# Four transformer blocks on one core: layer 0's spreads over two DMA queues, a limit on late pieces, a fifth early expert slot, and another order in the attention over heads

## Chip, core and metric

The kernel runs on one core of a Trainium2 chip. A core has TensorE (PE in the profile, with its weight loads PEld), VectorE (DVE), ScalarE (ACT), GpSimd (POOL) and SyncE (SP), each with an instruction stream of its own, in order. DMAs are issued from SP, ACT or POOL. The metric is the time of the kernel on the device in microseconds (us); smaller is better.

## The reference, cut to what matters

Four blocks work one after another on x (4 x 512 x 288, float32), all with layer norm, shift, scale and gates that are computed from a conditioning vector per batch, and 16 heads of 18 elements. Layers 1 and 3 differ from each other in nothing that matters here.

```python
# layer 0: attention over 512 tokens, then the best 2 of 4 experts per token
h = _modulate(_ln(x), sh_msa, sc_msa)
q, k, v = ...
attn = softmax(einsum('bhqd,bhkd->bhqk', q, k) * hd ** -0.5)
x = x + g_msa * (einsum('bhqk,bhkd->bhqd', attn, v) @ w_proj + b_proj)
xf = _modulate(_ln(x), sh_mlp, sc_mlp).reshape(-1, C)
topk_logits, topk_idx = top_k(xf @ w_gate, 2)
x = x + g_mlp * (sum over the two experts e of gates[e] * (gelu(xf @ w1[e] + b1[e]) @ w2[e] + b2[e]))
# layers 1 and 3: attention over tokens, then one MLP (288 -> 1152 -> 288)
# layer 2: attention over the 16 heads of each token, then one MLP
attn = softmax(einsum('nthd,ntkd->nthk', q * scale, k))       # 16 x 16 for each token
out = einsum('nthk,ntkd->nthd', attn, v)
out = out.transpose(0, 2, 1, 3).reshape(n, t, d)               # heads ahead of tokens
x = x + gate_msa * (out @ proj_w + proj_b)
```

## The kernel before

**One order, written by a planner.** The instructions of all engines are emitted in one order that the program works out itself. Around a backbone of loops stand lists of tasks: `products` (TensorE work), `lanes` (small DVE, ACT and POOL work), `moves` (scatters to memory), `loads`, `spreads` and `casts`. A task has a due time, keys that must be ready, and a generator that emits it piece by piece and yields the estimated cost of each piece. The planner's clock `flow["now"]` goes up by one at each `gap` (L152) of the backbone; it counts emission and not time. `fill` (L126) takes from a list what is ready, up to a budget in us; when the budget is used up it goes on as long as the open task, or the next, is past its due time (plus `SLACK`, 8, for lanes and moves). `mark(key, delay)` makes a key ready `delay` gaps later. A generator that yields `WAIT` gives up its turn until the next gap, one that yields `BANK` waits for a free bank of PSUM, and `Whole` marks the end of a unit of TensorE work.

**Two coroutine lists.** Where the stage of layer 2 runs beside the MLPs, `chain` (the tile loop) and `beside` (work next to it) are advanced by `follow` (L181) at each gap, against a credit that grows by 1.6 per gap. A bank that is free is offered to `beside` first and then to `chain` (L207).

**Token attention (layers 0, 1, 3).** Four batches times four units of four heads, 64 steps in all. Queries and keys come out of TensorE as packed rows `qc` (L640, ACT copy L666) and must be spread, so that each head starts at a partition of its own: `spread` (L686) issues one DMA for each head j and each half s (queries or keys), 19 rows of 512 elements, on SP, except the later heads of unit 0, which go out on ACT. Four buffers `spreads_of` rotate. A step computes scores (L711), takes their maximum on DVE (`mx`, L721), and six steps later (`LEAD`) the scores again, turned, with the exponential on ACT (`ex`, L749) and the product with the values (L777). `set_maxima` (L755) turns the maxima (L760), copies them on ACT (L762) and writes them into the unit's spread buffer by a DMA from POOL (L763). In the norm (L506) POOL computes the power for `rstd` (L528, or L520 to L523 where ACT does the scaling), and DVE (L543, L546, L548) or ACT (L537) scales. Each step ends with two gaps, in which the other tasks are emitted.

**Experts (layer 0).** When a batch's attention is done, `logits` (L1335) turns the normed rows `xh` (L1343) and multiplies them with the gate; then follow the choice of experts, places, and `scatter` (L1495), eight indirect DMAs from POOL (L1500) that write the rows to memory sorted by expert. The products run as 19 blocks of 256 rows (`expert_block`, L1690), each for one expert. The first `EARLY` (4) of them are blocks known to be full after two of the four batches, and load from a first list; the others need the list and the scatter of all batches. `SHORT` names two slots after them with 128 rows. `DONE` says after which block a batch's results can be gathered.

**Layer 2's attention over heads** runs on DVE, POOL and ACT beside the MLPs of layers 1 and 2. It goes over 16 tiles of 128 tokens (`stream`, L1153). For each tile, `kept` (L993) computes query, key and value by TensorE (L1002); the query stays in a bank, key and value images go to SBUF by ACT (L1011), into the first two thirds of the buffer `spreads_of[i % 4]`. `weigh` multiplies and sums on DVE (L1020, L1026), four groups a tile; the exponential is on ACT (L1193), `weighted` on POOL (L1039), `summed` on DVE (L1051), `finish` scales (L1064) and sends the result to memory. After four tiles `after` (L1130) reads the batch back with heads ahead of tokens, turns its rows (L1082), projects, and prepares the MLP's input; `before` (L1121) does the norm of the next batch. MLP work (L1916, gelu on ACT L1927, L1938) fills TensorE meanwhile.

Of the kernel before, what the change touches and what calls it, by code (L numbers as in the profile page):

```python
# [19 lines left out]
P = 128  # L20
# [30 lines left out]
INSIDE = (44, 56)  # L51
RATE = 1.6
SLACK = 8
EARLY = 4
SHORT = (EARLY + 1, EARLY + 3)
TRIOS = [[0, 1, 2], [3, 4, 5], [6, 7, 8]]
DUOS = [[0, 1], [2, 3], [4, 5], [6, 7], [8]]
# [3 lines left out]
def tile_dit_blocks(ctx: ExitStack, tc: tile.TileContext, x_in, cond_t, sel_den, sel_b, w_gate, layers, out):  # L61
# [25 lines left out]
    n_layers = len(layers)  # L87


    flow = {"now": 0, "turn": 0, "others": (6, 7), "credit": 0.0, "rate": 0.0}  # L90


    chain, beside = [], []
# [29 lines left out]
                return where.pop(i)  # L123
        return None

    def fill(where, started, us, slack=0):  # L126

        while True:
            if not started:
                item = take(where, us <= 0, slack)  # L130
                if item is None:
                    return us
                started.append(item)
            if us <= 0 and started[0][0] + slack > flow["now"]:
                return us
            try:
                took = next(started[0][2])
            except StopIteration:
                started.pop()
                continue  # L140
            if took is WAIT:
                return us
            us -= took

    def fill_others():
        fill(lanes, open_lane, 1.0, SLACK)
        fill(moves, open_move, 1.0, SLACK)
        fill(loads, open_load, 1000.0)
        fill(spreads, open_spread, 1000.0)
        fill(casts, open_cast, 1000.0)  # L150

    def gap(us):  # L152
        flow["now"] += 1
        before = flow["turn"]
        wanted = any(item[1] for item in chain + beside)
        fill(products, open_product, 0.0 if wanted else us)
        used = flow["turn"] != before or bool(open_product)
        fill_others()
        if chain or beside:
            close_all()  # L160
            follow(used)
# [22 lines left out]
    def follow(used):  # L184


        flow["credit"] = min(flow["credit"] + flow["rate"], 3.0)
        bank = [not used]

        def piece(item):  # L190
            if item[1]:
                if not bank[0]:
                    return False
                bank[0] = item[1] = False
            cost = next(item[0], None)
            if cost is None:
                (chain if item in chain else beside).remove(item)
                return False
            if cost is BANK:
                item[1] = True  # L200
                return piece(item)
            if cost is WAIT:
                return False
            flow["credit"] -= cost
            return True

        for item in beside + chain:  # L207
# [295 lines left out]
    xh, ht = {}, {}  # L503
    held = []

    def norm(l, half, b):  # L506
        key = (l, half, b)
        n = f"{l}_{half}_{b}"
        mv = small.tile([P, TB, 2], F32, tag="mv", name=f"mv_{n}")
# [7 lines left out]
        if scalar:  # L517

            off = small.tile([P, TB], F32, tag="off", name=f"off_{n}")
            nc.gpsimd.tensor_scalar_add(rstd, mv[:, :, 1], EPS)  # L520
            nc.gpsimd.tensor_tensor(rstd, rstd, minus_half, ALU.pow)
            nc.gpsimd.tensor_tensor(off, mv[:, :, 0], rstd, ALU.mult)
            nc.gpsimd.tensor_scalar_mul(off, off, -1.0)  # L523
            for _ in range(3):
                yield WAIT
        else:
            nc.vector.tensor_scalar_add(rstd, mv[:, :, 1], EPS)
            nc.gpsimd.tensor_tensor(rstd, rstd, minus_half, ALU.pow)  # L528
# [76 lines left out]
    def attention(l, start):  # L605
# [81 lines left out]
        def spread(u):  # L687

            b, g = divmod(u, NG)
            t = qk[u] = spreads_of[u % 4]  # L690
            for j in range(HG):
                for s in range(2):

                    at = g * UQ + (s * HG + j) * HO
                    end = at + HO
                    to = j * HP
                    while at < end:
                        m, r = divmod(at, P)
                        n = min(end - at, P - r)
                        queue = nc.scalar if u == 0 and j >= HG // 2 else nc.sync  # L700
                        queue.dma_start(t[to : to + n, s, :], packed[b, m][r : r + n, :])
# [136 lines left out]
        def steps(inside=None, tail=None):  # L838
# [9 lines left out]
            def sum_pair(step, to):  # L848
                sum_values(step - 1, to, True, False)
                sum_values(step, to, False, True)  # L850

            for step in range(first_step, N_STEPS + 1):
                odd = step % 2
                mark(("step", l, step), 0)
                if step < end:
                    flow["others"], flow["turn"] = ((4, 5, 6, 7) if odd and step > 0 else (0, 1, 2, 3)), -1
# [56 lines left out]
        for b in range(B):  # L913
# [3 lines left out]
            task(  # L917
                lanes, start - 70 if first else at_step(s0 - LEAD - 9 if b else s0 - LEAD - 6),
                [("x", l, 0, b)] + ([("scattered", B - 1)] if l == 1 else []) + ([("step", l, 0)] if b else []),
                norm(l, 0, b),  # L920
            )
            free = [("first products", l, b - 2)] if b >= 2 else []
            if prev == OVER_HEADS and b < 2:
# [58 lines left out]
    def attention_over_heads(l):  # L982
# [12 lines left out]
        def kept(i, s):  # L995

            b, t = tiles[i]
            h = ht[l, 0, b]
            to = QUERIES[i % 2][:, :C] if s == 0 else other()[:, :C]
            for k in range(NK):  # L1000
                n = KP + (1 if k == NK - 1 else 0)
                nc.tensor.matmul(  # L1002
                    to, h[:n, k, t * P : (t + 1) * P], w["wqkv"][:n, k, s * C : (s + 1) * C],
                    start=k == 0, stop=k == NK - 1,
                )
            if s == 1:
                qkv[i] = spreads_of[i % 4].rearrange("p s f -> p (s f)")[:, : 2 * C].rearrange(
                    "p (s h d) -> p s h d", s=2, d=HD
                )
            if s:  # L1010
                nc.scalar.activation(  # L1011
                    qkv[i][:, s - 1].rearrange("p h d -> p (h d)"), to, AF.Copy, scale=SCALE if s == 1 else 1.0
                )

        def weigh(i, g):
            hs = slice(g * GH, (g + 1) * GH)
            if g == 0:
                sc[i] = work.tile([P, NH, NH], F32, tag="hs", bufs=4, name=f"hs_{l}_{i}")
            prod = work.tile([P, GH, NH, HD], F32, tag="va", bufs=1, name=f"pq_{l}_{i}_{g}")
            nc.vector.tensor_tensor(  # L1020
                prod,
                QUERIES[i % 2][:, :C].rearrange("p (h d) -> p h d", d=HD)[:, hs, :].unsqueeze(2).to_broadcast([P, GH, NH, HD]),
                qkv[i][:, 0].unsqueeze(1).to_broadcast([P, GH, NH, HD]),
                ALU.mult,
            )
            nc.vector.tensor_reduce(sc[i][:, hs, :], prod, AX.X, ALU.add)  # L1026
# [7 lines left out]
        def weighted(i, g):  # L1034
# [4 lines left out]
            engine.tensor_tensor(  # L1039
                prod,  # L1040
                sc[i][:, hs, :].unsqueeze(2).to_broadcast([P, GH, HD, NH]),
                qkv[i][:, 1].rearrange("p h d -> p d h").unsqueeze(1).to_broadcast([P, GH, HD, NH]),
                ALU.mult,
            )
            pv[i, g] = prod
# [76 lines left out]
        def before(b):  # L1122

            yield from until(("x", l, 0, b))
            if b >= 2:
                yield from until(("first products", l, b - 2))
            yield from norm(l, 0, b)
            yield from turn_normed(0, b)

        def after(b):  # L1130
# [1 line left out]
            for _ in range(3 if b < B - 1 else 1):  # L1132
                yield WAIT
            read(b)
            for _ in range(6 if b < B - 1 else 3):
                yield WAIT
            yield from until(("gated", b))
            for k in range(NK):
# [3 lines left out]
            for t in range(TB):  # L1142
                yield BANK
                project(b, t)
                yield -1.5
            mark(("x", l, 1, b), 2)
            if b < B - 1:
                beside.append([gate_projection(b + 1), False])
            yield from until(("x", l, 1, b))
            yield from norm(l, 1, b)  # L1150
            yield from turn_normed(1, b)

        def stream():  # L1153
# [182 lines left out]
    def logits(b):  # L1336
        key = (0, 1, b)
        h = work.tile([P, NK, S], F32, tag="hm", bufs=4, name=f"hl_{b}")
        for k in range(KF + 1):
            n = P if k < KF else RC  # L1340
            to = other()
            for t in range(TB):
                nc.tensor.transpose(to[:n, t * P : (t + 1) * P], xh[key][:, t, k * P : k * P + n], ident)  # L1343
            nc.scalar.copy(h[:n, k, :], to[:n, :])
            yield Whole(0.43)
        pl = other()
        for k in range(KF + 1):
            n = P if k < KF else RC
# [147 lines left out]
    def scatter(b):  # L1496
        key = (0, 1, b)
        for t in range(TB):
            for s in range(2):
# [4 lines left out]
                unordered(i, "x_mem")  # L1504
                scatters.append(i)
                nc.gpsimd.memset(tick, 0.0)
                yield 0.5
        held.remove(key)
        mark(("scattered", b))

# [181 lines left out]
    def expert_block(i):  # L1692
# [517 lines left out]
```

## Time and profile before

| what | us |
|---|---|
| median of three runs (2243.33 to 2248.39) | 2246.33 |
| the profiled execution | 2245.67 |
| its span, first to last instruction | 2244.0 |
| TensorE busy | 2075.5 (92%) |
| DVE busy | 1066.5 (48%) |
| ACT busy | 815.7 (36%) |
| POOL busy | 503.7 (22%) |
| mean granted clock of TensorE | 0.961 |

The chain of work that ended last has 62% of the span on TensorE and 12% on DVE. In time, layer 0's attention takes about the first 440 us, the expert blocks the time to about 872, layer 1's attention to about 1290; layer 2's attention over heads runs from there to 1629 (its last L1064 at 1628.89), and the rest is the end of layer 2 and layer 3. An "idle before" in brackets at an instruction is the time that its engine stood still before it, with what released it.

### The profile page before, as it was taken

Reading aid. Unit: us, or ns where it says so; the run is one execution under the profiler, and the core shown is the slowest. Engines: PE = TensorE matmul, PEld = TensorE weight load, DVE = VectorE, ACT = ScalarE, POOL = GpSimd, SP = SyncE. Lnnn points to the kernel's source line nnn. Section 1 sums busy time; section 2 is a strip of 40 time slices with the busy share of each in tenths; the row PEclk is TensorE's granted clock in tenths of the full one; section 3 lists DMA queues with packets and bytes.
Section 4 is the critical chain, followed back from the end, with each engine's and each line's share of the span. In section 5 each row is a group of like instructions: output and inputs, shape, how many; then the busy total and the mean of one; then the engine's idle time right before and its main releaser. Section 6 shows DMA issues by size and latency. Waiting matters only on the chain.

```text
span 2244.0 us, 28773 instructions
## 1 busy us (share of the span) xinstructions
PE 2075.5 (92%) x10720; PEld 1159.9 (52%) x10720; DVE 1066.5 (48%) x1660; ACT 815.7 (36%) x1325; POOL 503.7 (22%) x516
## 2 busy tenths in 40 slices
PE   7899989889999998989999999979799999999998
PEld 2333434357777575344454466657556444444555
DVE  4556656632002403566534279798821355664111
ACT  2434433422222122545435422434312555546111
POOL 1101020231002203110000129788811201001010
PEclk9989998989999999999999999999899999999999
DMA  3244211425665453100000000210310100000000
GB/s 80 62 126 154 72 57 26 113 95 172 197 200 172 131 178 121 35 23 20 17 6 20 1 17 9 66 31 7 40 42 23 50 22 15 15 20 1 0 22 21
DMA packets 170957, 139.10 MB, mean 62 GB/s; under 512 B 79379, under 2 KB 152523, under 8 KB 170818
## 3 DMA queue, kind: packets, MB, share of 16 engines
q1 hardware_dynamic: 164670, 126.10, 19.6%
q0 software_dynamic: 5952, 10.85, 1.6%
q8 instruction: 85, 1.39, 0.3%
q14 instruction: 54, 0.44, 0.1%
q10 hardware_dynamic: 196, 0.31, 0.0%
HBM read 96.49 MB, written 26.00 MB: 55 GB/s over the span
## 4 chain that ended last, share of the span: by engine, by line
PE 62%; DVE 12%; issue 4%; DMA 3%; POOL 2%; ACT 2%; SPq 1%; another core or an unknown queue 0%; POOLq 0%; ACTq 0%; DVEq 0%
PE banks L711 11%; PE banks L640 7%; PE banks L1730 7%; PE banks L1710 6%; PE banks L1879 5%; PE banks L1856 4%; PE banks L777 4%; PE banks L828 3%; PE banks L1938 3%; DVE mx L721 3%; PE banks L1916 2%; DVE pq L1020 2%; DVE ho L1051 2%; DVE hs L1026 2%; DMA qk<-qc 1%
## 5 line engine op out<-in xcount | busy, mean ns | idle before, releaser
L721 DVE TENSOR_REDUCE mx<-banks 128x4 f32<-128x2048 f32 (+1 forms) x354 | 423.6, 1238 | 353.0 <-PE banks L711 310.3
L749 ACT ACTIVATE ex<-banks 128x1024 f32<-128x1024 f32 (+1 forms) x471 | 377.9, 865 | 318.2 <-PE banks L711 312.8
L711 PE MATMUL banks<-qk 32*128 32x512 f32 x3072 | 442.3, 634 | 39.9 <-DVE mx L721 19.2
L711 PEld LDWEIGHTS banks<-qk 32*128 32x128 f32 x3072 | 168.2, 187 | 218.0 <-issue 83.0
L777 PE MATMUL banks<-ex,va 128*32 128x512 f32 x1536 | 193.1, 616 | 2.7 <-ACT ex L749 2.5
L1039 POOL TENSOR_TENSOR pv<-hs,qk 128x1152 f32<-128x1152 f32 x60 | 190.6, 3192 | 8.0 <-ACT hs L1193 7.9
L1730 PE MATMUL banks<-w_b,hid_b 128*128 128x288 f32 x648 | 178.2, 418 | 0.0
L640 PE MATMUL banks<-ht,wqk 96*128 96x512 f32 (+1 forms) x348 | 167.7, 615 | 9.2 <-DVE mx L721 8.1
L1710 PE MATMUL banks<-block,w_b 128*128 128x256 f32 (+1 forms) x684 | 154.8, 372 | 0.6 <-ACT hid_b L1722 0.6
L1722 ACT ACTIVATE hid_b<-banks,b_b 128x256 f32<-128x256 f32 (+1 forms) x171 | 66.8, 461 | 241.2 <-PE banks L1716 134.5
L1730 PEld LDWEIGHTS banks<-w_b,hid_b 128*128 128x128 f32 x648 | 117.2, 190 | 49.8 <-issue 23.5
L1916 PE MATMUL banks<-ht,w 128*128 128x256 f32 x432 | 113.9, 396 | 25.7 <-ACT hid L1927 25.3
L1710 PEld LDWEIGHTS banks<-block,w_b 128*128 128x128 f32 x684 | 123.9, 192 | 25.2 <-issue 7.4
L1938 PE MATMUL banks<-w,hid 128*128 128x288 f32 x432 | 130.5, 436 | 0.0
L763 POOL DMA_DIRECT2D qk<-maxima x48 | 29.6, 617 | 446.3 <-ACT maxima L762 381.6
L640 PEld LDWEIGHTS banks<-ht,wqk 96*128 96x128 f32 (+1 forms) x348 | 61.4, 187 | 101.3 <-issue 57.9
L777 PEld LDWEIGHTS banks<-ex,va 128*32 128x32 f32 x1536 | 40.2, 111 | 140.7 <-issue 73.7
L599 POOL TENSOR_TENSOR x<-x,upd_a 128x288 f32<-128x288 f32 x48 | 38.6, 804 | 320.1 <-DVE upd_a L598 300.3
L1879 PE MATMUL banks<-w,hid 128*128 128x288 f32 x432 | 108.8, 410 | 0.0
L1916 PEld LDWEIGHTS banks<-ht,w 128*128 128x128 f32 x432 | 83.0, 197 | 46.4 <-ACT hid L1927 28.5
L596 DVE TENSOR_TENSOR upd_m<-banks,b 128x576 f32<-128x576 f32 x12 | 9.1, 754 | 205.9 <-PE banks L1879 205.9
L1856 PE MATMUL banks<-ht,w 128*128 128x512 f32 x216 | 100.4, 612 | 5.0 <-ACT hid L1872 4.5
(243 smaller groups left out, 2503.0 us busy)
## 6 DMA issues: line engine op xcount, KB each, us to landing
w_b<-in_w SPq DMA_DIRECT2D x57, 432.0 KB
w_b<-in_w SPq DMA_DIRECT2D x57, 384.0 KB
qk<-qc SPq DMA_DIRECT2D x316, 38.0 KB
wa<-in_wada SPq DMA_DIRECT2D x24, 288.0 KB
x_mem<-zeros SPq DMA_DIRECT2D x21, 256.0 KB
y_mem<-zeros SPq DMA_DIRECT2D x21, 256.0 KB
block<-x_mem SPq DMA_DIRECT2D x17, 288.0 KB
y_mem<-y_b SPq DMA_DIRECT2D x17, 288.0 KB
```

What stands on the lines that cost most here:

```text
L640: nc.tensor.matmul(to, st(rows, k), mv(rows, k), start=k == 0, stop=k == NK - 1)
L711: nc.tensor.matmul(to, qk[u][r, of, c * P : (c + 1) * P], qk[u][r, 1 - of, :], start=True, stop=True)
L721: nc.vector.tensor_reduce(mxs[u % 2][:, j : j + n, c], banks[:, bank + j : bank + j + n, :], AX.X, ALU.max)
L749: nc.scalar.activation(ex[step, j // 2][:, j % 2 : j % 2 + n, :], banks[:, to[j] : to[j] + n, :], AF.Exp, scale=SCALE)
L777: nc.tensor.matmul(to[j * HP : (j + 1) * HP, :], vas[0][:, c, at : at + HP], ex[step, j // 2][:, j % 2, :], start=first, stop=last,)
L1039: engine.tensor_tensor(prod, sc[i][:, hs, :].unsqueeze(2).to_broadcast([P, GH, HD, NH]), qkv[i][:, 1].rearrange("p h d -> p d h").unsqueez ...
L1710: nc.tensor.matmul(banks[:, UP + j, cols], w1[:, k, j * P : (j + 1) * P], hx[i][:, k, cols], start=k == 0, stop=False)
L1730: nc.tensor.matmul(banks[:, PY + t, :C], hid[j][:, t * P : (t + 1) * P], w2[:, j, :], start=f == 0, stop=f == NF - 1)
L1856: nc.tensor.matmul(banks[:, 4 + j, :], full[:, k, (f % 3) * P : (f % 3 + 1) * P], h[:, k, :], start=k == 0, stop=False,)
L1879: nc.tensor.matmul(banks[:, t, :C], hf[:, t * P : (t + 1) * P], w["w2"][f // 3][:, f % 3, :], start=f == 0, stop=f == NF - 1,)
L1916: nc.tensor.matmul(banks[:, UP + j, :BT], full[:, k, (f % 3) * P : (f % 3 + 1) * P], h[:, k, s], start=k == 0, stop=False,)
L1938: nc.tensor.matmul(banks[:, PY + t, :C], hf[:, t * P : (t + 1) * P], w["w2"][f // 3][:, f % 3, :], start=False, stop=f == NF - 1,)
```

## The change

Five parts. The first early expert slots are five and not four, which moves `SHORT` and `DONE` too. In layer 0, the half s = 1 of every spread goes out on POOL's queue. Lanes and moves that are late stop in a gap after 0.8 us over their budget in attention steps (`least`), until two steps before the end of the look-ahead; products that are late stop at 0.05 over it in expert blocks (`most`); a scatter is counted as 1.0 and the last batch's turned rows in `logits` as 0.6. In `follow`, the free bank is offered to `chain` first. In the over-heads stage key images lie in the first third of their buffer, value images in the second and third by turns of four tiles; the norm ahead of layer 3 waits 10 gaps between POOL and ACT instead of 3, that of layer 2's batches 2 and 3 waits 6; `after` waits 13 gaps (9 in the last batch) before it turns rows, where it was 6 (3); and the next batch's gated projection is taken up after the norm rather than ahead of it.

```diff
-EARLY = 4
+EARLY = 5
 SHORT = (EARLY + 1, EARLY + 3)
...
-    def fill(where, started, us, slack=0):
+    def fill(where, started, us, slack=0, least=-1e9):
...
-            if us <= 0 and started[0][0] + slack > flow["now"]:
+            if us <= least or us <= 0 and started[0][0] + slack > flow["now"]:
                 return us
...
-        fill(lanes, open_lane, 1.0, SLACK)
-        fill(moves, open_move, 1.0, SLACK)
+        fill(lanes, open_lane, 1.0, SLACK, flow["least"])
+        fill(moves, open_move, 1.0, SLACK, flow["least"])
...
-        fill(products, open_product, 0.0 if wanted else us)
+        fill(products, open_product, 0.0 if wanted else us, 0, flow["most"])
...
-        for item in beside + chain:
+        for item in chain + beside:
             if item[1]:
                 piece(item)
...
-    def norm(l, half, b):
+    def norm(l, half, b, lag=3):
...
-            for _ in range(3):
+            for _ in range(lag):
                 yield WAIT
...
-                        queue = nc.scalar if u == 0 and j >= HG // 2 else nc.sync
+                        queue = nc.scalar if u == 0 and j >= HG // 2 else nc.gpsimd if l == 0 and s else nc.sync
...
+            flow["least"] = -0.8
             for step in range(first_step, N_STEPS + 1):
                 odd = step % 2
+                if step == end - 2:
+                    flow["least"] = -1e9
...
-                norm(l, 0, b),
+                norm(l, 0, b, 10 if first and prev == OVER_HEADS else 3),
...
-            if s == 1:
-                qkv[i] = spreads_of[i % 4].rearrange("p s f -> p (s f)")[:, : 2 * C].rearrange(
-                    "p (s h d) -> p s h d", s=2, d=HD
-                )
             if s:
-                nc.scalar.activation(
-                    qkv[i][:, s - 1].rearrange("p h d -> p (h d)"), to, AF.Copy, scale=SCALE if s == 1 else 1.0
-                )
+                third = 0 if s == 1 else 1 + i // 4 % 2
+                mine = spreads_of[i % 4].rearrange("p s f -> p (s f)")[:, third * C : (third + 1) * C]
+                nc.scalar.activation(mine, to, AF.Copy, scale=SCALE if s == 1 else 1.0)
+                qkv[i, s] = mine.rearrange("p (h d) -> p h d", d=HD)
...
-            yield from norm(l, 0, b)
+            yield from norm(l, 0, b, 3 if b < 2 else 6)
             yield from turn_normed(0, b)
...
-            for _ in range(6 if b < B - 1 else 3):
+            for _ in range(13 if b < B - 1 else 9):
                 yield WAIT
...
+            yield from until(("x", l, 1, b))
+            yield from norm(l, 1, b)
             if b < B - 1:
                 beside.append([gate_projection(b + 1), False])
-            yield from until(("x", l, 1, b))
-            yield from norm(l, 1, b)
             yield from turn_normed(1, b)
...
-            yield Whole(0.43)
+            yield Whole(0.43 if b < B - 1 else 0.6)
...
-                yield 0.5
+                yield 1.0 if b < B - 1 else 0.5
...
+        flow["most"] = -0.05
         for g, fs in enumerate(TRIOS):
             hid = up(g, fs)
...
+        flow["most"] = -1e9
```

More of the change, by code (lines that the diff above doesn't have):

```diff
@@ L87, in tile_dit_blocks @@
     n_layers = len(layers)
-    flow = {"now": 0, "turn": 0, "others": (6, 7), "credit": 0.0, "rate": 0.0}
+    flow = {"now": 0, "turn": 0, "others": (6, 7), "credit": 0.0, "rate": 0.0, "least": -1e9, "most": -1e9}
     chain, beside = [], []
@@ L1022, in weigh @@
                 QUERIES[i % 2][:, :C].rearrange("p (h d) -> p h d", d=HD)[:, hs, :].unsqueeze(2).to_broadcast([P, GH, NH, HD]),
-                qkv[i][:, 0].unsqueeze(1).to_broadcast([P, GH, NH, HD]),
+                qkv[i, 1].unsqueeze(1).to_broadcast([P, GH, NH, HD]),
                 ALU.mult,
@@ L1041, in weighted @@
                 sc[i][:, hs, :].unsqueeze(2).to_broadcast([P, GH, HD, NH]),
-                qkv[i][:, 1].rearrange("p h d -> p d h").unsqueeze(1).to_broadcast([P, GH, HD, NH]),
+                qkv[i, 2].rearrange("p h d -> p d h").unsqueeze(1).to_broadcast([P, GH, HD, NH]),
                 ALU.mult,
```

## The prediction

> **What bounds the kernel now.** I read the page first, then what TensorE waited for, then busy time by stretch, and last the order in time around the long waits.
>
> ```profile
> PE 2075.5 (92%) x10720; PEld 1159.9 (52%) x10720; DVE 1066.5 (48%) x1660; ACT 815.7 (36%) x1325; POOL 503.7 (22%) x516
> ```
>
> TensorE (PE) is busy for 2075.5 of 2244.0 us. The change takes no matmul away, so it can only act on the 168.5 us in which PE is idle and on the time in which its clock is low. The waits of PE say who ended the idle time (total us, times, longest):
>
> ```profile
> PE banks L1916 <- ACT hid L1927: 25.3, 8, 11.3
> PE banks L711 <- DVE mx L721: 19.2, 13, 5.0
> PE banks L640 <- DVE mx L721: 16.3, 10, 5.2
> PE banks L581 <- ACT xh L537: 12.5, 3, 10.5
> ```
>
> The first and the fourth belong to the over-heads stage (layer 2), the others to token attention, where DVE's maximum L721 sets PE's banks free. Busy time by stretch says where it is lost (after the stretch: its length, then busy time of PE, PEld, DVE, ACT and POOL, granted clock, DMA share, GB/s):
>
> ```profile
> 108.00:130.00 22.00, 13.66 (x48) 3.71 (x41) 3.01 (x3) 2.63 (x5) 0.64 (x1) 0.61 0.51 146
> ...
> 275.00:440.00 165.00, 141.36 (x819) 58.65 (x815) 101.79 (x248) 63.98 (x94) 29.52 (x52) 0.90 0.26 68
> 440.00:530.00 90.00, 77.52 (x366) 50.36 (x363) 35.35 (x151) 27.14 (x49) 28.30 (x47) 0.91 0.33 106
> ...
> 1290.00:1450.00 160.00, 148.25 (x627) 107.17 (x624) 129.27 (x136) 47.78 (x90) 102.80 (x60) 0.93 0.13 30
> 1450.00:1630.00 180.00, 152.24 (x654) 110.52 (x653) 166.47 (x179) 73.16 (x131) 155.61 (x92) 0.92 0.18 27
> ```
>
> These five hold 83.97 us of PE's idle time, half of all of it, and every one has a clock below 0.94, while 530 to 872 us has 1.00 and 905 to 1290 us 0.98. So a stall costs itself and a slow stretch after it; I price the clock as (1 - clock) x length.
>
> **The spread over two queues.** In layer 0, the second 19 rows of each head pair (66 DMAs) go out from POOL instead of SP. This is the one spread of layer 0 that came late:
>
> ```profile
> 108.30 6.17 SPq L701 DMA_DIRECT2D qk<-qc  x9
> ...
> 114.47 2.04 PE L711 MATMUL banks<-qk 32*128 32x512 f32 x2 [6.01 <-DMA qk<-qc]
> ...
> 122.70 2.04 PE L711 MATMUL banks<-qk 32*128 32x512 f32 x2 [1.02 <-DMA bada<-in_bada]
> ```
>
> Its first rows are used 6.2 us after the first issue, its last ones 14.4 us after. PE stood or ran slowly from 108.46 to 124.74, for eight matmuls that took 1.14 just before: 15.1 us lost. With half of the pieces on another queue I let the 8.2 us between first and last rows halve: 4.1, and 1 for the clock, so -5. Bounds: 0 if the pieces land no sooner (the DMA engines are 51% busy there), -15 if all of it goes. The Trainium skill ("DMA: Bandwidth & Descriptors", Issuing engines are not separate DMA queues) speaks against it: queues of several engines share the same 16 DMA engines, and only the time to issue is saved. By that rule it would be four issues of 0.69 us, about -3 and not -5, and the sum 2 us smaller.
>
> POOL pays for it: 66 issues at the 0.594 us that its own qk<-maxima takes (median of 48) are 39 us, in a layer where POOL works 18.28 of the first 108 us and 29.52 of 275 to 440. That idle time hides them. Not hidden is what stands behind them in POOL's order: the norm's power L528, for which DVE waits 15.9 us in 13 places already, and the maxima rows L763, each behind up to five pieces (3.0 us). L763 has two attention steps to spare; of L528 four are in reach, and I charge +3 in all (0 to +12: four times 3.0). Two units of the last batch have their pieces behind four scatters L1500 each (0.97 us, 1.28 apart: 5 us); two steps of some 9 us cover that, and without this cover a spread would cost like the one above.
>
> **Late pieces limited, chain before the rest.** In attention steps, late DVE and copy pieces now stop after about three in a gap, until two steps before the end; late products stop in expert blocks. Between 275 and 440 us PE is idle for 23.6 us and loses 16.5 to the clock, 40 in all. The waits there that name DVE are 3.63, 1.43, 0.88, 1.57, 1.03, 1.33, 0.87, 2.29 and 1.11 us; the first stands behind eight scalings of the norm (L543, L546) between two maxima. They sum to 14.1. I let half of it go (7), and of the clock's 16.5 a quarter (4): -11. Bounds: -25 if all 14.1 and two thirds of the clock go; +5 if the pieces only gather at the layer's end. A wait of 4.98 near 333 us names no cause, and stays. At 872 to 905 (PE busy 22.94 of 33) 1.3 us of statistics move behind the copies: -2 (0 to -6).
>
> **The fifth early slot.** The block products start with five blocks known to be full, so block 4 no longer waits for the last batch's list; that batch's routing transposes come some nine small gaps later.
>
> ```profile
> 485.68 0.48 PE L1343 MATMUL banks<-ident,xh 128*128 128x128 f32 x1 [4.96 <-DVE xh L546]
> ...
> 524.79 1.11 PE L1682 MATMUL banks<-ident,block 128*128 128x128 f32 x4 [3.03 <-DMA block<-x_mem]
> ```
>
> The first waits for a norm that sat behind POOL's eight scatters of the batch before (472.76 to 482.76; the power L528 starts at 482.81); three waits of 0.51 follow it. The second waits for rows that the last scatter wrote. Together 9.5 us of the stretch's 12.5 idle; of its 8.1 of clock the same share is 6.2. Sum 15.7. As the transposes now stand later, the list of the last batch comes later too, by about 9 us; block 5, which needs it, comes a block of about 18 us later. So cover is left, but not much: -13 (-18 to 0; with the cover gone, 5 of wait come back).
>
> **The over-heads stage.** K's image now lies in a third of its own and V's alternates, so no image waits for the weighting of the tile four before; images come before the turning of finished rows; norm scalings wait 6 or 10 gaps, turning 13 or 9 instead of 6 or 3.
>
> ```profile
> 1470.81 0.41 ACT L1011 ACTIVATE qk<-banks 128x288 f32<-128x288 f32 x1 [7.56 <-POOL pv L1039]
> ...
> 1476.19 2.00 PE L581 MATMUL banks<-ident,xh 128*96 128x128 f32 x4 [10.48 <-ACT xh L537]
> ...
> 1585.22 2.07 PE L1916 MATMUL banks<-ht,w 128*128 128x256 f32 x4 [11.28 <-ACT hid L1927]
> ```
>
> ACT is in order: while an image waits for POOL (7.56), or a scaling for the norm's offset (11.14 at 1579.38), the gelu L1927 behind it waits, and PE with it. These two stalls (21.8) with 25.6 for the clock (11.2 and 14.4) are most of what the stage loses. But DVE is busy for 166.47 of 180 us in its second half, so the chain over tiles can shorten there by 13.5 at most, and in the first half mainly by the 13.70 for which DVE waits for tile 8's query product (until 1445.73). Against it: later turning keeps layer 2's MLP from PE. One half of a batch is 20.4 us of PE (L1916 and L1938: 113.9 + 130.5 over 12 halves), and I count one half moved behind the chain's end, now 1628.89. If the chain ends 16 earlier and the moved half takes 9 of that back, PE reaches layer 3's first turn about 7 earlier: -7. Bounds: -21 (chain 16, 5 of clock) to +20 (the whole half behind an end that stays).
>
> **The sum.** -5 + 3 - 11 - 2 - 13 - 7 = -35. Token attention of layers 1 and 3 keeps PE's order: nothing. From the profiled execution's 2245.67 that is 2210.7; the median is 0.66 above it: 2211.
>
> **Rivals.** *Only part pays*: DVE keeps the stage's pace (0 for -7), and half of the -11 returns later: -5 + 3 - 6 - 13 = -21, 2225. For it: DVE at 92% there. Against: the two long stalls hang on order, not on DVE's load.
> *The stage pays in full*: -21 there, -20 in 275 to 440, -15 and -2 in the others, -5 + 3: -60, 2186. For it: 57% of the stage's loss is clock, which goes with the stalls. Against: the second half has no DVE slack.
> *Late turning starves PE* (the slower one): around 1465 to 1490 PE has no MLP piece ready, since batch 0's rows are turned later, for about 28 us of DVE work instead of 11 (rows' durations added up in the new order): +17, +5 of clock after it, +20 for the half moved behind the chain's end, -7 for half of DVE's wait at tile 8: +35. With -28 from the rest: 2253. It decides once the chain's end gains nothing on the stage's start (339 us from 1290 to 1629) while the MLP of batch 0 starts over 198 us after that start (188 now). For it: PE has only images (1.6 us per six matmuls) between. Against: images that come sooner shorten the chain itself.
> *It doesn't do what it says*: layer 0's pieces land as late from POOL, the limit only shifts lateness, and the fifth block's cover is used up: 2246.
>
> **How the numbers follow.** Forecast 0.48, part 0.22, full 0.10, nothing 0.06, starved 0.14. Within 0.2% is 4.5 us to each side, about what this can tell from no change. Faster: 0.48 + 0.22 + 0.10 = 0.80; same 0.06; slower 0.14. The forecast's own range is 2195 to 2230. The range takes in the part case, the nothing case and the nearer half of the full one, and leaves out the starved one: 2187 to 2247.
>
> **What would show it.** Right: no 6 us wait on qk<-qc near 108 and a clock above 0.8 there; no wait above 2 us at L1343 and L1682; L1011 no longer waiting for POOL; the chain's end (L1064) near 1585 (1629, less 28 from layer 0 and 16 of its own); L1916 and L581 together below 20 us (37.8 now). Wrong: new waits of DVE for rstd above 3 us, PE L711 waiting for pieces behind L1500, or PE idle for more than 15 us before batch 0's MLP in layer 2 with its first matmul later than the image of tile 9.

## The result, and the profile after

| | us |
|---|---|
| before, median of six runs (2243.33 to 2255.24) | 2246.49 |
| after, median of six runs (2211.59 to 2231.18) | 2225.89 |
| after, the profiled execution (span 2218.2) | 2220.06 |

The changed kernel takes 0.9897 of the time before (95% interval 0.9873 to 0.9922): 18 to 29 us less. The forecast was 35 less, 2211. Its runs lie further apart (19.6 us) than those before (11.9).

First the page's engine line of the changed kernel, then what its TensorE waited for (total us, times, longest):

```profile
PE 2057.7 (93%) x10720; PEld 1152.7 (52%) x10720; DVE 1072.6 (48%) x1660; ACT 813.0 (37%) x1324; POOL 535.2 (24%) x582
```

```profile
PE banks L1918 <- ACT hid L1929: 27.9, 8, 6.3
PE banks L581 <- ACT xh L537: 14.8, 3, 14.4
PE banks L640 <- DVE mx L721: 14.4, 12, 4.1
PE banks L711 <- DVE mx L721: 12.8, 10, 2.5
PE banks L423 <- DMA wa<-in_wada: 7.3, 1, 7.3
PE banks L1687 <- DVE block L1675: 7.1, 2, 5.2
```

The two waits of the over-heads stage (gelu, now L1929, and scaled rows) are no smaller: 42.7 together against 37.8. The waits for DVE's maxima went from 35.5 to 27.2. L1343 (6.5 before) and L1682 (3.0) are off the top, and a new wait stands at L1687. Busy time by stretch, cut at the same places of the work as in the view before (its length, then PE, PEld, DVE, ACT, POOL, granted clock, DMA share, GB/s):

```profile
108.00:130.00 22.00, 18.29 (x54) 5.52 (x58) 6.95 (x13) 3.70 (x5) 3.88 (x9) 0.69 0.72 199
...
270.00:420.00 150.00, 136.79 (x850) 57.25 (x850) 101.78 (x244) 66.66 (x98) 39.39 (x71) 0.98 0.25 64
420.00:510.00 90.00, 79.19 (x384) 54.11 (x376) 34.91 (x152) 26.14 (x49) 28.18 (x47) 0.98 0.44 139
...
1266.00:1426.00 160.00, 146.34 (x630) 105.99 (x627) 142.49 (x148) 50.89 (x94) 111.70 (x63) 0.95 0.12 23
1426.00:1592.00 166.00, 138.26 (x595) 101.55 (x594) 157.92 (x165) 61.50 (x112) 136.32 (x79) 0.91 0.22 36
```

The end of layer 0's attention is 15 us shorter (150 where it was 165), and its clock is 0.98 where it was 0.90. The last row is 14 us shorter (166 for 180): the chain over tiles has its last row (L1064) at 1589.5 for 1628.9, 39.4 sooner, of which 23.7 is the stage's sooner start and 15.7 its own. Yet PE's idle time in the last two rows together is 41.4, against 39.5 before.

### The profile page after: what moved, and what is told of

Same layout as the page of the kernel before. It is cut to its first block, busy times and chain, and to the rows that moved or that the text cites. A ratio compares the mean times of both kernels' runs of the same rounds, so it can differ in the third digit from the quotient of the medians.

```text
span 2218.2 us, 28814 instructions
## 1 busy us (share of the span) xinstructions
PE 2057.7 (93%) x10720; PEld 1152.7 (52%) x10720; DVE 1072.6 (48%) x1660; ACT 813.0 (37%) x1324; POOL 535.2 (24%) x582
## 3 DMA queue, kind: packets, MB, share of 16 engines
q1 hardware_dynamic: 163370, 123.92, 19.6%
## 4 chain that ended last, share of the span: by engine, by line
PE 55%; DVE 12%; POOL 3%; issue 3%; ACT 2%; DMA 1%; ACTq 0%; POOLq 0%; SPq 0%; DVEq 0%
PE banks L711 11%; PE banks L640 7%; PE banks L1730 6%; PE banks L1710 5%; PE banks L1881 5%; PE banks L1858 4%; PE banks L777 4%; DVE pq L1020 2%; DVE ho L1051 2%; PE banks L828 2%; PE banks L1940 2%; POOL pv L1039 2%; DVE mx L721 2%; DVE hs L1026 2%; PE banks L1918 2%
## 5 line engine op out<-in xcount | busy, mean ns | idle before, releaser
L711 PE MATMUL banks<-qk 32*128 32x512 f32 x3072 | 441.1, 628 | 30.9 <-DVE mx L721 12.8
L711 PEld LDWEIGHTS banks<-qk 32*128 32x128 f32 x3072 | 167.8, 185 | 208.4 <-issue 78.5
L1710 PE MATMUL banks<-block,w_b 128*128 128x256 f32 (+1 forms) x684 | 157.6, 377 | 4.1 <-ACT hid_b L1722 4.1
L1918 PE MATMUL banks<-ht,w 128*128 128x256 f32 x432 | 117.1, 407 | 28.5 <-ACT hid L1929 27.9
L1710 PEld LDWEIGHTS banks<-block,w_b 128*128 128x128 f32 x684 | 125.8, 195 | 29.3 <-issue 6.8
L1940 PE MATMUL banks<-w,hid 128*128 128x288 f32 x432 | 125.5, 423 | 0.0
L599 POOL TENSOR_TENSOR x<-x,upd_a 128x288 f32<-128x288 f32 x48 | 38.6, 804 | 315.2 <-DVE upd_a L598 293.1
L777 PEld LDWEIGHTS banks<-ex,va 128*32 128x32 f32 x1536 | 40.0, 110 | 138.1 <-issue 70.4
L1881 PE MATMUL banks<-w,hid 128*128 128x288 f32 x432 | 108.8, 410 | 0.0
```

The costliest lines, as they stand in the source:

```text
L711: nc.tensor.matmul(to, qk[u][r, of, c * P : (c + 1) * P], qk[u][r, 1 - of, :], start=True, stop=True)
L777: nc.tensor.matmul(to[j * HP : (j + 1) * HP, :], vas[0][:, c, at : at + HP], ex[step, j // 2][:, j % 2, :], start=first, stop=last,)
L1710: nc.tensor.matmul(banks[:, UP + j, cols], w1[:, k, j * P : (j + 1) * P], hx[i][:, k, cols], start=k == 0, stop=False)
L1881: nc.tensor.matmul(banks[:, t, :C], hf[:, t * P : (t + 1) * P], w["w2"][f // 3][:, f % 3, :], start=f == 0, stop=f == NF - 1,)
L1918: nc.tensor.matmul(banks[:, UP + j, :BT], full[:, k, (f % 3) * P : (f % 3 + 1) * P], h[:, k, s], start=k == 0, stop=False,)
L1940: nc.tensor.matmul(banks[:, PY + t, :C], hf[:, t * P : (t + 1) * P], w["w2"][f // 3][:, f % 3, :], start=False, stop=f == NF - 1,)
```

## Experiments

Each run undoes or does one part, or a set of parts. Times are medians, and the ratio is to the kernel before, run beside it on the same chip, with its 95% interval. Beside spread_only, early_only, late_only and heads_only the kernel before took 2245.58; beside least_only, rest_only, no_early and old_turning 2246.74; beside the other four 2239.36. So runs of different groups are compared by their ratios.

| run | what it is | us | ratio to before |
|---|---|---|---|
| spread_only | only the second queue | 2245.35 | 0.9993 [0.9976, 1.0011] |
| early_only | only the fifth slot | 2245.44 | 0.9996 [0.9981, 1.0012] |
| late_only | only the limits and costs of late pieces | 2231.65 | 0.9939 [0.9914, 0.9964] |
| least_only | of these, the limit in attention steps | 2246.22 | 0.9998 [0.9981, 1.0016] |
| rest_only | of these, all but that limit | 2231.69 | 0.9953 [0.9927, 0.9980] |
| yields_only | of these, the two costs alone | 2224.35 | 0.9911 [0.9879, 0.9942] |
| heads_only | only the over-heads parts | 2238.05 | 0.9973 [0.9952, 0.9993] |
| rest_heads | rest_only and heads_only | 2227.76 | 0.9931 [0.9903, 0.9959] |
| no_early | the whole change, four slots | 2224.39 | 0.9886 [0.9846, 0.9926] |
| old_turning | the whole change, old lags before turning | 2244.91 | 0.9985 [0.9959, 1.0010] |
| stats_sooner | rest_heads, statistics sooner | 2224.49 | 0.9910 [0.9880, 0.9941] |
| stats_sooner_lags | the same, shorter lags | 2227.60 | 0.9930 [0.9899, 0.9962] |

Whole times move by several us from run to run, so I also cut every trace at the same instructions. Each row below is one execution, the profiled one, and the same work differs there too: the end of layer 0's attention takes 154.1 in rest_only and 161.7 in rest_heads, whose edits up to there are the same. The columns are us between them: the spread (fourth to fifth copy of maxima, L762), the same two copies on (sixth to seventh), the end of layer 0's attention (tenth to sixteenth), from there to the second block's result (L1738), from there to the thirteenth, from there to the last, and the over-heads stage (first weighing to layer 2's last MLP copy).

| run | spread | 6-7 | end L0 | first blocks | to 13th | to last | over heads |
|---|---|---|---|---|---|---|---|
| before | 38.6 | 27.5 | 165.6 | 107.5 | 207.3 | 136.5 | 466.6 |
| after | 36.1 | 25.5 | 150.5 | 94.8 | 203.6 | 151.5 | 465.2 |
| spread_only | 35.8 | 23.8 | 162.8 | 107.4 | 207.4 | 148.4 | 469.5 |
| early_only | 38.3 | 27.9 | 161.7 | 107.3 | 198.2 | 152.0 | 469.6 |
| late_only | 38.8 | 30.2 | 155.2 | 94.7 | 212.7 | 138.7 | 469.3 |
| least_only | 38.4 | 29.6 | 159.9 | 107.5 | 207.2 | 145.2 | 470.2 |
| rest_only | 39.0 | 28.2 | 154.1 | 94.7 | 212.7 | 138.5 | 467.1 |
| yields_only | 38.9 | 27.4 | 158.3 | 89.6 | 208.8 | 149.0 | 465.7 |
| heads_only | 38.8 | 27.9 | 162.6 | 107.1 | 207.2 | 135.9 | 465.2 |
| rest_heads | 38.6 | 30.1 | 161.7 | 94.8 | 212.6 | 138.1 | 465.3 |
| no_early | 34.4 | 23.8 | 150.5 | 94.8 | 212.7 | 151.1 | 465.2 |
| old_turning | 34.8 | 23.8 | 150.4 | 93.1 | 204.7 | 154.4 | 488.0 |
| stats_sooner | 38.4 | 27.3 | 157.5 | 98.4 | 212.7 | 138.6 | 461.3 |
| stats_sooner_lags | 38.7 | 28.0 | 160.6 | 97.5 | 211.0 | 143.2 | 458.6 |

### The second queue alone

```diff
-queue = nc.scalar if u == 0 and j >= HG // 2 else nc.sync
+queue = nc.scalar if u == 0 and j >= HG // 2 else nc.gpsimd if l == 0 and s else nc.sync
```

> Only the second queue for layer 0's spreads. Theory: the late spread near 108 us ends about 3 us sooner and the slow clock after it is a little shorter; 4 to 6 us in all, about 2241, and DVE's wait for the first scores after the spread goes from 18.4 to about 15. Rival (the forecast's term): 5 us at the spread alone and 3 given back by POOL. Rival 2: the pieces land as late as before, within 2 us of 2246.

The place gets better: the spread's column is 34.4 to 36.1 in the four kernels with the second queue and 38.3 to 39.0 in the ten without it. The changed kernel's order in time there:

```profile
105.99 2.57 POOL L701 DMA_DIRECT2D qk<-qc  x5
...
106.56 2.73 SPq L701 DMA_DIRECT2D qk<-qc  x4
...
111.60 8.09 PE L711 MATMUL banks<-qk 32*128 32x512 f32 x8 [4.85 <-DMA qk<-qc]
...
119.79 2.29 DVE L721 TENSOR_REDUCE mx<-banks 128x4 f32<-128x2048 f32 x1 [15.05 <-PE banks L711]
```

The same maximum in the kernel before:

```profile
124.85 2.29 DVE L721 TENSOR_REDUCE mx<-banks 128x4 f32<-128x2048 f32 x1 [18.40 <-PE banks L711]
```

SP is done issuing after 2.73 us instead of 6.17, and DVE waits 15.05 instead of 18.40: about the time to issue, and no more. The eight matmuls still crawl (8.09 us). The column 6-7 is better too, by some 4 us, in these four kernels and in no other. There PE's waits at L423 for conditioning weights (wa), 0.9 to 2.7 us in the ten traces without the second queue, are missing (the 7.3 in the waits of the changed kernel is the program's first load and stays); that SP's queue has fewer pieces ahead of that load is the likely reason. Idle time and slow clock account for about 3 of these 4 us. So the two places gain some 6, but the whole time of this run does not move. Its trace lost 11.9 us in the blocks (148.4 for 136.5) with no change of work there: 10.2 of it in 20.5 us at a clock of 0.50. That this happens in most runs and not only in the profiled one is not shown.

### The fifth slot alone

```diff
-EARLY = 4
+EARLY = 5
```

> Only the fifth early slot. Theory: PE's waits of 4.96 (L1343) and 3.03 (L1682) go, with their slow clock: 13 to 16 us gained by the end of block 0; but results of a batch are gathered one block later, and the combine of batch 0 then stands on DVE ahead of a block's copy near 770 us, which gives 5 to 6 us back: about 2237. Rival: nothing is given back, about 2232. Rival 2: the wait near 770 us comes from another part, and is not there in this run.

The second half of the theory held, the first fell. What PE waited for in this run:

```profile
PE banks L1343 <- DVE xh L546: 6.6, 4, 5.0
PE banks L1687 <- DVE block L1675: 5.2, 1, 5.2
PE banks L1682 <- DMA block<-x_mem: 3.0, 1, 3.0
```

Both old waits are there, unchanged, and the new one of 5.2 at L1687 has come. The rows that wait at L1682 are those of the fourth block, not the fifth: 19 loads and 19 turnings, counted through, put the turning at 524.8 in the kernel before at the fourth place. It had been an early slot all along. A block's load is made to wait for every scatter emitted ahead of it, and the fourth load stood behind all 32. The last scatter and the fourth load in the kernel before (in this run it is the same):

```profile
518.61 1.15 POOL L1500 DMA_INDIRECT x_mem<-xh,places  x1 [0.19 <-issue]
521.48 0.62 SPq L1639 DMA_DIRECT2D block<-x_mem  x1
```

So the planner's order decided, not the number of slots. The columns show the rest: 9.1 us less up to the thirteenth result (work moved back by one block), 15.5 more after it.

### The limits and costs of late pieces, together

```diff
+flow["least"] = -0.8     # attention steps; fill(...) for lanes and moves stops there
+flow["most"] = -0.05     # expert blocks; fill(...) for products stops there
-yield Whole(0.43)        # turned rows in logits
+yield Whole(0.43 if b < B - 1 else 0.6)
-yield 0.5                # a scatter
+yield 1.0 if b < B - 1 else 0.5
```

> Only the limits on late pieces, with the costs of scatter and of the last turned rows. Theory: the waits of PE for DVE's maxima between 275 and 440 us shrink, 10 to 15 us: about 2233. Rival: the pieces gather at the end of layer 0's attention and give it back: within 4 us of 2246. The trace shows it by the times at which the maxima of steps 40 to 64 are copied.

14 us, as expected, and nothing gathers at the layer's end. But the waits at L1343 and L1682 shrank in this run as well (to 2.0 and 1.2 us in all), which the theory had given to the fifth slot. So I took this part to pieces.

### The limit in attention steps, and the rest without it

```diff
+flow["least"] = -0.8     # least_only: this and its use in fill
+flow["most"] = -0.05     # rest_only: this, and the two costs
```

> Only the limit on late lanes and moves in attention steps. Theory: it frees PE from waits for DVE's maxima between 275 and 440 us, about 7 us (the gain of the three limits together by 420 us), and leaves the waits of 5.0 (L1343) and 3.0 (L1682) near 485 and 525 us: 2238 to 2241. Rival: it carries the whole 14 us of the three: about 2232.

> The limit on late products in expert blocks, the scatter counted as 1.0 and the last turned rows as 0.6, without the limit in attention steps. Theory: these move the load of the fourth block ahead of the last batch's scatters and the last routing transposes behind their norm, so that the waits of 5.0 and 3.0 go with their slow clock: about 7 us, 2238 to 2241, and the waits between 275 and 440 us stay. Rival: nothing, since the waits only move: 2246.

The limit that the change's words put first is worth nothing alone (0.9998), against theory and rival both. The others carry it, and more of it than that run's theory said (0.9953, about 11 us): the waits between 275 and 440 us, which were to stay, shrink as well. The row of busy times over the column "end L0" in least_only, and then in rest_only:

```profile
256.26:416.13 159.87, 139.75 (x869) 59.73 (x863) 104.87 (x243) 64.05 (x94) 29.88 (x54) 0.96 0.20 49
```

```profile
253.80:407.90 154.10, 138.46 (x869) 59.98 (x863) 101.67 (x226) 63.83 (x93) 27.32 (x50) 0.97 0.20 47
```

PE is idle there for 20.1 us with the limit alone (19.7 to 20.9 in the four traces without any of the parts on late pieces) and for 15.6 with the others. The rest of the differences in this column is granted clock.

### The two costs alone

```diff
-yield Whole(0.43)
+yield Whole(0.43 if b < B - 1 else 0.6)
-yield 0.5
+yield 1.0 if b < B - 1 else 0.5
```

> Only two numbers: a scatter counts 1.0 and not 0.5 in the first three batches, and the last batch's turned rows 0.6 and not 0.43. Theory: spacing the scatters is what counts, since two of them in a gap delay the spreads and scores around 330 us and the norm behind them; this run has most of the 11 to 14 us of the larger sets: about 2235, with the 5.0 wait at L1343 and the 4.98 near 335 us smaller. Rival: the limit on late products in expert blocks is what counts, and this run stays at 2244 or more.

Two numbers in the planner give as much as the whole change, as far as this can tell: 0.9911 against 0.9897, intervals that overlap. The theory holds against the rival, and it named only half: PE's longest wait for a maximum at L711 falls (from 5.0 to 2.5 us), PE's idle time over "end L0" is 15.3, and the expert blocks gain as well. What each of the two numbers does alone was not run. This run's order in time around the places where PE had stood:

```profile
469.09 0.70 SPq L1639 DMA_DIRECT2D block<-x_mem  x1
...
472.31 0.63 PE L1682 MATMUL banks<-ident,block 128*128 128x128 f32 x4 [0.27 <-DMA block<-x_mem]
...
475.69 0.60 PE L1343 MATMUL banks<-ident,xh 128*128 128x128 f32 x4
...
483.98 0.62 SPq L1639 DMA_DIRECT2D block<-x_mem  x1
...
496.04 1.09 POOL L1500 DMA_INDIRECT x_mem<-xh,places  x1 [26.41 <-DVE arena L1464]
```

The first load is that of the third block, and its turning at L1682 stands ahead of the last batch's L1343, so that PE has work while POOL and DVE make the normed rows; L1343 waits for nothing. The second load, the fourth block's, goes out at 483.98, 12 us ahead of the last batch's first scatter (496.04). Before, it came after the last of them.

The column "first blocks" falls from 107.5 to 89.6. With the limit on late products added (rest_only, late_only) it is 94.7, and the way to the thirteenth result takes 212.7 instead of 208.8. By these traces that limit costs some 9 us, of which 4.8 are idle time of PE (a wait of 3.5 for ACT at L1710 stands in all eight kernels with it); a kernel with all parts but this one was not run.

### The over-heads parts alone

```diff
-for item in beside + chain:
+for item in chain + beside:
...
+third = 0 if s == 1 else 1 + i // 4 % 2
...
-for _ in range(6 if b < B - 1 else 3):
+for _ in range(13 if b < B - 1 else 9):
```

(with the longer norm lags and the later gated projection)

> Only the parts in the over-heads stage (images' banks first, value images by turns, longer lags). Theory: the chain over the tiles ends about 13 us sooner, but PE waits about as long as before, and layer 3 starts within 3 us: 2243 to 2247. Rival (the forecast's term): 7 us faster, about 2239. Rival (late turning starves PE): slower, 2255 or more.

The time says 2 to 11 us faster, which fits the forecast's 7 as well. The stage's own column says 3: 465.2 to 465.3 in the four kernels with all of these parts, 465.7 to 470.2 (mean 468.3) in the seven without. These 3 us are granted clock (25.6 us lost to it in the four, 27.3 to 29.0 in the seven); PE's idle time over the stage is 46.5 to 46.8 in the four and 43.3 to 48.5 in the seven. In the changed kernel the chain does end 15.7 sooner; the PE side of it is this wait:

```profile
1452.39 0.45 DVE L512 BATCH_NORM_STATS2 st<-x 128x6 f32<-128x288 f32 x1
...
1456.81 2.18 ACT L537 ACTIVATE xh<-x,off,rstd 128x288 f32<-128x288 f32 x4 [13.85 <-POOL off L523]
...
1457.49 2.88 PE L581 MATMUL banks<-ident,xh 128*128 128x128 f32 x8 [14.39 <-ACT xh L537]
```

That is the slower rival's starved PE, 14.4 where it was 10.5. The projected rows were written at 1438.76 (L1094), but their statistics stand on DVE behind three groups of weighing.

### Adding up, and taking the slot or the lags back out

```diff
-EARLY = 5                                            # no_early
+EARLY = 4
-for _ in range(13 if b < B - 1 else 9):              # old_turning
+for _ in range(6 if b < B - 1 else 3):
```

> The set without the limit in attention steps (late products, scatter 1.0, turned rows 0.6) with the over-heads parts, on SP's queue alone and with four early slots. Theory: the parts left out are worth nothing, and the sums of the single runs hold: 2246.5 less 11 to 15 less 7.5, so 2224 to 2228, the same as the whole change (2226). Rival: the parts left out are worth 5 us or more together with the others, and this run is at 2231 or more.

> The changed kernel with four early slots instead of five. Theory: the fifth slot gives nothing, and its later combine costs a wait of 5.2 at L1687 near 773 us: without it 0 to 6 us faster than the changed kernel's 2226, so 2220 to 2226. Rival (the forecast's term): the fifth slot is worth 13 us once the other parts are in, and this run is at 2235 or more.

> The changed kernel with the old lags before turning (6 and 3 gaps, not 13 and 9). Theory: the MLP of layer 2's first batch starts sooner, PE's wait of 14.4 near 1457 us shrinks or goes, and the half of an MLP batch moved behind the chain's end comes back: 3 to 8 us faster than 2226. Rival: turning early puts the rows' DMA and the ACT copies in the way of the tile chain, as before the change, and the kernel is slower than 2226.

The first two agree with the theory. Without the second queue, the fifth slot and the limit in attention steps the ratio is 0.9931, where rest_only and heads_only add up to 0.9926, and its interval overlaps that of the whole change. But the two lie 0.34% (7.6 us) apart, so that the parts left out are worth nothing is not shown; the rival's 5 us are not excluded. With four slots it is 0.9886 for 0.9897: the rival's 13 us for the fifth slot are. The third went to the rival by its time; its mechanism is half of it. The chain's end does come later (its last L1064 is 327.0 us after the first weighing, 320.1 in the changed kernel), but most is this: with the old lags PE reaches L1082 before the rows are back from memory:

```profile
1397.58 0.36 SPq L1069 DMA_DIRECT2D rows<-scratch  x1
...
1402.02 0.66 PEld L1082 LDWEIGHTS banks<-ident,rows 128*96 128x96 f32 x4 [10.11 <-DMA rows<-scratch]
1402.02 1.09 PE L1082 MATMUL banks<-ident,rows 128*96 128x128 f32 x4 [9.71 <-DMA rows<-scratch]
```

Four such waits (9.7, 3.2, 3.2, 8.4; 24.6 in all) make the stage 22.8 longer. Before the change 6 and 3 gaps were enough. That with images first a gap holds less PE work, so that the same count of gaps is less time, is the likely reason; no run changes the order alone. By this the longer lags are no loss to weigh against the images: they are what the new order needs.

### Statistics sooner, and lags fitted

```diff
-mark(("x", l, 1, b), 2)
+mark(("x", l, 1, b), 0)                              # both
-for _ in range(13 if b < B - 1 else 9):
+for _ in range((12, 10, 10, 8)[b]):                  # stats_sooner_lags
```

> As rest_heads, and the statistics of layer 2's second norm are taken up as soon as the batch's rows are projected (delay of 2 gaps made 0): on DVE they stand ahead of two groups of weighing, about 8 us sooner. Theory: PE's wait of 14.4 us at L581 for the scaled rows is DVE's order, so it shrinks by some 8 us and the kernel is 3 to 9 us faster than rest_heads. Rival: the time is filled by the chain's end anyway, or DVE now waits for the projected rows, and it is the same within 3 us or slower.

> As stats_sooner, with the gaps before turning at 12, 10, 10 and 8 for the four batches, not 13, 13, 13 and 9. Theory: with 6, 6, 6 and 3 gaps PE waited 9.7, 3.2, 3.2 and 8.4 us for the rows to come back from memory; these lags sit just behind that, so no wait at L1082 above 1 us and up to 4 us faster than stats_sooner. Rival: the rows come later here, L1082 waits again, and it is slower.

PE's wait for the scaled rows, in rest_heads and then in stats_sooner:

```profile
PE banks L581 <- ACT xh L537: 14.8, 3, 14.4
```

```profile
PE banks L581 <- ACT xh L537: 8.2, 3, 7.8
```

It shrinks by 6.6 us, the stage by 4.0, and with the shorter lags by 2.7 more (458.6), with no wait at L1082. Whole times can't show this: 2227.76, 2224.49 and 2227.60, in one group, have ratios with intervals that overlap.

## Why the prediction came out as it did

The direction held: stalls of PE went, and slow clock with them. But the sum was 35 and 18 to 29 came, and its largest term was put under the wrong edit. Term by term:

- **Second queue, -5 and +3 for POOL.** At the spread -3.4 (means 35.3 and 38.7 of the two groups), not -5. The Trainium skill ("DMA: Bandwidth & Descriptors", Issuing engines are not separate DMA queues) says that only the time to issue is saved. The trace agrees: SP's issuing there is 3.44 us shorter and DVE's wait 3.35. I had not seen the gain at the conditioning weights. POOL cost nothing: DVE waited 15.7 us for the power L528 in 14 places, 15.9 in 13 before, and the 66 issues took 0.516 us each (median). The two places gain some 6, the whole run alone nothing.
- **Late pieces, -11 and -2.** Size nearly right, cause wrong. The end of layer 0's attention is 15.1 shorter in the changed kernel and 10.4 in late_only. I gave it to the limit in attention steps, which is worth nothing alone; the count of a scatter and of the last turned rows, to which I gave no price, moves it. Of the -2 where the next layer starts, PE's idle time shows half: 9.0 of 33 us (847 to 880) for 10.1.
- **Fifth slot, -13.** This is the step that failed: "block 4 no longer waits for the last batch's list". The wait was the fourth block's, already early, for scatters that the planner had emitted ahead of its load; and the wait at L1343 has nothing to do with the slots. The slot alone shows no gain (0.9996). The changed kernel does gain 12.7 at this place ("first blocks"), but by the costs (17.9 in yields_only): that the size of the term came true is luck.
- **Over-heads stage, -7.** -3 by the stage's column, 2 to 11 by time. The chain gained 15.7, just the 16 allowed; of that the stage kept 1.4 in the changed kernel (465.2 for 466.6) and 3 by the means, with PE waiting where the MLP should be. L1011 no longer waits for POOL (19.2 us in four places before, none after), as the step said. "Late turning starves PE" was half right: the wait is there, but 6.6 of its 14.4 us come from the statistics' place on DVE, the rest stays open, and turning sooner costs 22.8. The rival that pays in full has 57% of the stage's loss in the clock; by its own rows it is 39% (25.6 beside 39.5 of idle time).
- **The later expert blocks**, at nothing in the sum, cost 11.3 in the profiled pair (the two columns from the second result to the last: 355.1 for 343.8). Two waits are new there: 3.5 at L1710, in every kernel with the limit on late products, and 5.2 at L1687, in every kernel with five slots. Slow clock adds 5.1. With the 5.6 missing in the over-heads stage, this is where the sum fell short.

What the forecast's own test asked for: the chain's end near 1585 (1589.5; layer 0 and the blocks gave 23.7 of the 28), no wait above 2 us at L1343 and L1682 (true, but not by the slot), no wait of 6 us on qk<-qc near 108 (4.85), a clock above 0.8 at 108 to 130 (0.69), the two over-heads waits below 20 us (42.7).

## What to carry to other kernels

A wait in the trace names the engine that let go, not the edit that will free it: count which block, batch or tile stands there before you put a gain under an edit. Where a planner lays out the order, the cost that it assumes for a step (a scatter at 0.5 or 1.0) can matter more than the rules built around it, and a lag counted in steps must be fitted again when the steps change their length. Run parts alone, and cut the traces at fixed instructions: stats_sooner shows 4 us in its stage where the whole times show nothing.

## What the runs showed of the hardware

The granted clock can drop after a short wait and stay low under full load. In yields_only, from 740 to 764 us, PE was busy nearly throughout; its one wait was 0.78 us (at 740.91, L711 for a maximum), and yet:

```profile
734.00:740.00 6.00, 6.00 (x22) 2.47 (x20) 2.18 (x4) 0.00 (x0) 3.84 (x4) 1.00 0.50 144
740.00:744.00 4.00, 3.22 (x6) 1.46 (x6) 2.67 (x4) 0.00 (x0) 0.00 (x0) 0.65 0.70 201
744.00:748.00 4.00, 4.00 (x9) 1.67 (x9) 1.23 (x2) 0.00 (x0) 0.00 (x0) 0.50 0.66 201
...
760.00:764.00 4.00, 4.00 (x13) 3.14 (x12) 2.95 (x7) 0.59 (x1) 0.00 (x0) 0.50 0.12 19
```

Half the clock for 23.9 us, some 12 us lost, in work that runs at 1.00 in the kernel before. The column "to last" shows it across the traces: 135.9 to 138.7 in six of them, 143.2 to 154.4 in eight. Two of the eight, spread_only and then the changed kernel:

```profile
726.06:874.46 148.40, 144.49 (x615) 96.75 (x613) 24.94 (x44) 28.82 (x68) 21.72 (x21) 0.93 0.45 137
```

```profile
697.50:849.00 151.50, 144.68 (x645) 97.86 (x643) 30.70 (x53) 30.31 (x69) 22.99 (x23) 0.98 0.43 132
```

Five of the eight have four slots, and slow clock takes 5.1 to 13.7 us there, 0 to 1.7 in the six. The three with five slots have more work in this column (some 30 matmuls more: x645 for x615) and the wait at L1687, and only 3.4 to 5.1 of clock. In the four-slot kernels it is the largest difference between these traces that no edit explains, and in spread_only's trace it took more than the second queue gained.

The clock records of all fourteen traces have two values, 0.50 and 1.00. The drops of a trace lie on one grid of 3.41 us, and every slow stretch but the last of a run, which the end cuts off, is a whole number of 3.41 us long: seven for the 23.9 us here. So one short wait costs 1.7 us of clock or several times that. PE's idle time alone does not decide: in yields_only drops follow 3.41 us with 0.63 to 0.78 of idle time, and others with 1.81 are followed by none. The Trainium skill ("TensorE: Matmul & The Clock Gate", What's actually happening) ties a drop to an idle window of about 3.4 us and the release to as much busy time. The length of the window agrees with these traces; neither condition fits these rows. What sets the drop off, and why it lasted, stays open.
